# Swapping the places of a search's two products in the attention loop of a two-layer graph network

## The chip, the cores and the metric

The kernel runs on one core of a Trainium2 chip. The metric is the device time of one execution in microseconds (us); lower is better. Five engines work side by side and meet through semaphores: TensorE (PE in the profile; its weight loads, PEld, are shown apart), VectorE (DVE), ScalarE (ACT), GpSimd (POOL) and SyncE (SP), which issues the DMAs.

## The reference

Two layers act on 3327 nodes of 128 features with a dense adjacency matrix. Layer 0 is a masked cosine attention; layer 1 is an attention that has 128 heads of only 8 features each, with the adjacency added twice to the scores. Cut to what matters here:

```python
    def _L1_gnn_ref(x, spatial_encoding, edge_encoding, Wq, Wk, Wv, Wo):
        ...
        q = (x @ Wq.T).reshape(d, n, h)
        k = (x @ Wk.T).reshape(d, n, h)
        v = (x @ Wv.T).reshape(d, n, h)
        a = jnp.einsum('dnh,dmh->dnm', q, k) * scale
        a = a + spatial_encoding + edge_encoding
        a = jax.nn.softmax(a, axis=2)
        out = jnp.einsum('dnm,dmh->dnh', a, v)
...
    x = _layernorm(x + _L0_gnn_ref(x, adj, L0_gnn_beta), axis=-1)
    x = _layernorm(x + _L1_gnn_ref(x, adj, adj, L1_gnn_Wq, L1_gnn_Wk, L1_gnn_Wv, L1_gnn_Wo), axis=-1)
```

Here d is 128 (the heads of layer 1), n is 3327 and h is 8. Every head has its own 3327 x 3327 matrix of scores, each row of which goes through a softmax. The softmax is made safe by subtracting, from each query's scores, the largest product of that query with any key. Finding this largest product is called the search below.

## The kernel before

**Tiling.** The nodes are padded to 3328, which is 26 tiles of 128 (`T`). Queries are taken in blocks of three tiles (384 queries). There are nine blocks; the first eight are full, and the ninth has two tiles. Heads are taken four at a time, so there are 32 groups. One block with one group is a unit; there are 9 x 32 = 288 units, the first 256 of them in full blocks. A unit goes through the 26 key tiles, one step of the main loop (L901) for each. That is 7,488 steps, 6,656 of them in full blocks.

**Rows of the array.** A head's 8 features, split into high and low parts, take 32 rows. Head a of the group lies in rows 32a to 32a+31 (`rows`, L239), so matmuls of different heads use different row groups of TensorE and run side by side. Matmuls of one head queue up in its row group.

**What one step computes.** Scores are made with keys on the partitions and queries along the free axis, for four heads. Two heads go into the two banks of `eb`, the other two into two tiles `ea`.

- `shifts` (L829, matmul at L832) starts a bank with the negated maximum of each query.
- `scores` (L836, L838) adds the products of keys and queries.
- For `eb`, ACT takes the exponential (L938), and POOL multiplies the result by the exponential of twice the adjacency (L939).
- For `ea`, TensorE adds twice the adjacency itself (`add_adj`, L815, eight matmuls at L819 that use all rows and 32 columns each), and ACT takes the exponential of each head (L963).
- `weigh` (L847, eight matmuls at L849) multiplies the weights of two steps before with the values and accumulates them in `acc`.

**The search.** While a unit is weighed, the maxima of later units are searched for (33 steps ahead). In full blocks each step has two pieces of it, made by `max_steps` (L242): a *pair*, which is one chunk of 512 keys against 128 queries for two heads (`max_pair`, L284: two matmuls into the two banks of tile `m2`, and one DVE reduction at L291 over 1024 columns), and a *single*, the same for one head (`max_single`, L306: one matmul into tile `m1`, one reduction at L312 over 512 columns). The single's head is never one of the pair's two. Chunk 6 holds only 256 keys, so a pair or single of that chunk is made of products of two query tiles or units (L302, L316). The searched unit's finished maxima are turned into shifts by `shift_parts` and three small transposes (`shift_turn`, L805), which three of each 26 steps carry.

**Banks.** All eight PSUM banks are in use: `ea` has two (a new step needs both back), `eb` two, `m2` two, `m1` one, `acc` one. So each product waits for the reader of the step before: the pair's matmuls for the reduction L291, the single's for L312, the shifts of `eb` for L938 and those of `ea` for L963.

**Order.** The four engines run in the order in which the program is written (`manual_schedule`); nothing reorders it. In a full-block step, TensorE's order is: shifts of `eb`, pair, scores of `eb`, shifts of `ea`, single, scores of `ea`, (shift turns), `add_adj`, `weigh`. DVE reduces the pair and then the single. The heads of `eb` (`hs_b`, L923) are the two that the pair doesn't use, so shifts and scores of `eb` have two row groups and the pair has the other two.

In the ninth block's search (`behind`, L914) both pieces are singles and follow the scores of `eb`.

Of the kernel before, what the change touches and what calls it, by code (L numbers as in the profile page):

```python
# [46 lines left out]
def gnn_two_layers(  # L47
# [188 lines left out]
    class Banks:  # L236
        pair = single = None
# [85 lines left out]
    def search(step):  # L323
        if step is not None:
            (max_pair if len(step[1]) == 2 else max_single)(*step)
# [16 lines left out]
    def max_step(k):  # L342

        i, j = divmod(k, 2 * T)
        if 2 * i >= NU:
            return None
        if j == 0:
            steps[i] = max_steps(2 * i, 2 * i + 1)
        return steps[i][j]

    def first_max(k):
        pair, single = max_step(k)
        max_pair(*pair)
        max_single(*single)
        if k == T:
            shift_parts(us[0])
# [415 lines left out]
    with ExitStack() as at:  # L772
# [15 lines left out]
        def load_values(u):  # L788

            u.vt = vts[u.i % 3]  # L790
            for first, n, rows in ((0, 112, T), (112, P - 113, T), (P - 1, 1, N - (P - 1) * T)):
                nc.sync.dma_start(
                    u.vt.rearrange("p g t r -> p g (t r)")[first : first + n, :, : rows * R9],
                    bass.AP(
                        tensor=v_s.tensor,
                        offset=v_s.offset + (4 * u.g * N + first * T) * R9,
                        ap=[[T * R9, n], [N * R9, 4], [1, rows * R9]],
                    ),
                )
            u.cx = sm.tile([P, QB], BF16, name="cx")  # L800

        def shift_turn(u, q, dst, start):
            for h in range(4):
                r = slice(32 * h, 32 * h + 32)
                nc.tensor.matmul(  # L805
                    dst[r],
                    parts[u.i % 2][:, q, h],
                    unit,
                    start=start,
                    stop=True,  # L810
                    tile_position=(0, 32 * h),
                    skip_group_check=True,
                )
# [58 lines left out]
        with tc.manual_schedule(  # L872
            engines={
                mybir.EngineType.PE,
                mybir.EngineType.Activation,
                mybir.EngineType.DVE,
                mybir.EngineType.Pool,
            }
        ):
            for i in range(2):  # L880
                load_values(us[i])
            for k in range(k_first, T + AHEAD):
                first_max(k)
            pp = at.enter_context(tc.tile_pool(name="at_p", bufs=6))
            seen = []
            acc = ps_o.tile([P, 512], F32, name="acc")
            nc.vector.memset(acc, 0.0)
            one = fix.tile([P, P], BF16, name="one")
            nc.vector.tensor_copy(one, ones)

            def new_a():
                return [ps_a.tile([P, 512], F32, name="ea") for _ in range(2)]

            e = ps_b.tile([P, 2, 512], F32, name="eb")
            for q in range(QT):
                shift_turn(us[0], q, e[:, 0, q * P : (q + 1) * P], True)
            nc.scalar.copy(us[0].cx, e[:, 0, :QB])  # L897

            todo = []
            turn = []  # L900
            for s in range(NU * T + LAG):  # L901
                i, j = divmod(s, T)
                u = us.get(i)
                if u is not None:
                    if j == 2 and i + 2 < NU:
                        load_keys(new_unit(i + 2))
                        load_queries(us[i + 2], own.tile([P, QB], F32R, name="qx"))
                        load_values(us[i + 2])
                    if j == 12 and i + 4 < G4:
                        gather(i + 4)  # L910
                    k = s + T + AHEAD
                    pair, single = max_step(k) or (None, None)

                    behind = pair is not None and len(pair[1]) == 1  # L914
                    if behind and Banks.pair is not None:
                        Banks.pair = None
                        search_banks.close()
                        ps_n = at.enter_context(tc.tile_pool(name="at_n", bufs=3, space=PSUM))
                        Banks.single = lambda: ps_n.tile([P, 512], F32, name="m3")
                    if behind:  # L920
                        hs_b = pair[1] + single[1]
                    else:
                        hs_b = (2, 3) if pair is None else tuple(  # L923
                            h for h in range(4) if h not in pair[1]
                        )
                    hs_a = tuple(h for h in range(4) if h not in hs_b)

                    e_b = ps_b.tile([P, 2, 512], F32, name="eb")
                    b01 = [e_b[:, x] for x in range(2)]
                    shifts(u, b01, hs_b)  # L930
                    if not behind:
                        search(pair)
                    scores(u, j, b01, hs_b, True)
                    if behind:
                        search(pair)
                        search(single)
                    pt_b = pp.tile([P, 2, QB], F32, name="pb")
                    nc.scalar.activation(pt_b[:, :, : u.nq], e_b[:, :, : u.nq], AF.Exp)  # L938
                    nc.gpsimd.tensor_tensor(  # L939
                        pt_b[:, :, : u.nq],  # L940
                        pt_b[:, :, : u.nq],
                        eT[:, j, : u.nq].unsqueeze(1).to_broadcast([P, 2, u.nq]),
                        ALU.mult,
                    )
                    e_a = new_a()
                    shifts(u, e_a, hs_a)
                    if not behind:
                        search(single)
                    scores(u, j, e_a, hs_a, False)
                    free = e_a[0][:, QB:]  # L950
                    x = us.get(i + 1)
                    copies = []
                    q = j - (T - 4)
                    if x is not None and 0 <= q < x.nt:
                        shift_turn(x, q, free, False)
                        copies.append(
                            lambda: nc.scalar.copy(x.cx[:, q * P : (q + 1) * P], free)
                        )
                    pt_a = pp.tile([P, 2, QB], F32, name="pa")
                    for h, e in enumerate(e_a):  # L960
                        add_adj(e, u, j)
                    for h, e in enumerate(e_a):
                        nc.scalar.activation(pt_a[:, h, : u.nq], e[:, : u.nq], AF.Exp)  # L963
                    for f in copies:
                        f()
                    if x is not None and not x.b:
                        order_keys(x, j)
                        if j == T - 1:
                            keep_keys(x)
                    pts = {}  # L970
                    for x in range(2):
                        pts[hs_a[x]], pts[hs_b[x]] = pt_a[:, x], pt_b[:, x]
                    todo.append((u, j, pts))
                    seen.append((pt_a, pt_b))
                    if len(seen) == 2:
                        a, b = seen.pop(0)
                        if s % 4 == 2:
                            met = sm.tile([P, 1], F32, name="met")
                            nc.scalar.activation(met, b[:, 0, 0:1], AF.Identity, bias=a[:, 0, 0:1])  # L979

                    if k % (2 * T) in (T, 2 * T - 1):
                        v = us.get(k // (2 * T) * 2 + (k % (2 * T) > T))
                        if v is not None:
                            shift_parts(v)
                if s >= LAG:
                    w = todo.pop(0)
                    weigh(*w)
                    if w[1] == T - 1:
                        take(us.pop(w[0].i))

                if turn and turn[0][0] <= s:
                    exp_adj_tile(*turn.pop(0)[1:])
                if u is not None and i + 1 < NU and units[i + 1][0] != u.b:
                    load_adj_tile(u.b + 1, j)
                    turn.append((s + 5, u.b + 1, j))
# [98 lines left out]
```

## Time and profile before

| | |
|---|---|
| median of 3 runs (lowest to highest) | 15163.88 us (15163.75 to 15168.83) |
| profiled execution | 15166.36 us |
| its span, from the first to the last instruction | 15164.6 us |
| mean granted TensorE clock | 0.996 of full speed |
| first shift of `eb` in the timeline | 774.61 us |
| first `eb` shift of the ninth block (128x256 tiles) in the timeline | 13908.37 us |
| mean step in the full blocks: 13133.76 us over 6,656 steps | 1.973 us |

Two costs per step, from the table of the costliest groups (mean of one, over the whole program):

| engine, line | work | mean ns |
|---|---|---|
| DVE L291 | reduction of a pair | 1226 |
| DVE L312 | reduction of a single | 682 |
| ACT L938 | exponential of `eb` | 788 |
| ACT L963 | exponential of one head of `ea` (two a step) | 479 |
| POOL L939 | product with the adjacency's exponential | 1766 |

A busy share says little here: PE is 99% busy, DVE 92%, POOL 91% and ACT 86%. Since matmuls overlap and their ends are modelled, a busy PE is not one at its peak. What sets the length of a step has to be read from the order of events inside a step.

### The profile page before, as it was taken

The page shows a single profiled execution, that of the slowest core. Times are in us where ns is not written, and L with a number is a line of the kernel's source. Part 1 is how long each engine was busy: PE and PEld are TensorE (multiplying, and loading weights), DVE is VectorE, ACT ScalarE, POOL GpSimd, SP SyncE. Part 2 cuts the span into 40 slices and gives each one's busy share as a digit, 9 for nine tenths or more (in the row PEclk, how much of TensorE's full clock was granted, in tenths as well). Part 3 has the DMA queues.
Part 4 walks back from the last instruction along what each step waited for, and adds up shares of the span by engine and source line. Part 5 has one row for each costly group of instructions (what it writes and reads, how often), then busy time and mean ns, then how long its engine had stood idle before and what let it go on. Part 6 is the DMA issues. An engine that isn't in the chain of part 4 may idle for free.

```text
span 15164.6 us, 489663 instructions
## 1 busy us (share of the span) xinstructions
PE 15016.7 (99%) x210460; PEld 6659.0 (44%) x210460; DVE 13878.7 (92%) x16267; ACT 13046.2 (86%) x27285; POOL 13765.4 (91%) x8925
## 2 busy tenths in 40 slices
PE   7899999999999999999999999999999999999999
PEld 5544444444444444444444444444444444444556
DVE  8899999999999999999999999999999999998997
ACT  7699999888888888888888888888888888888887
POOL 3489999999999999999999999999999999999998
PEclk9999999999999999999999999999999999999999
DMA  5622221111111111111111111111111111111222
GB/s 199 216 96 104 98 97 60 47 53 47 57 50 47 54 51 50 53 47 52 55 47 53 47 59 49 47 53 52 54 49 47 53 54 50 50 47 62 66 70 86
DMA packets 548935, 996.33 MB, mean 66 GB/s; under 512 B 147881, under 2 KB 492454, under 8 KB 500422
## 3 DMA queue, kind: packets, MB, share of 16 engines
q1 hardware_dynamic: 546758, 965.00, 19.3%
q8 instruction: 1648, 27.00, 0.7%
q14 instruction: 529, 4.33, 0.1%
HBM read 826.75 MB, written 192.54 MB: 67 GB/s over the span
## 4 chain that ended last, share of the span: by engine, by line
PE 96%; DVE 1%; ACT 1%; issue 1%; POOL 1%; DMA 0%; SPq 0%; DVEq 0%; POOLq 0%; ACTq 0%
PE acc L849 31%; PE ea L819 22%; PE m L276 17%; PE eb L832 13%; PE ea L832 8%; PE ea L838 1%; PE ea L805 1%; PE eb L838 1%; PE sc L394 1%; PE acc L527 0%; PE tp L135 0%; DVE kx L489 0%; ACT aT L439 0%; DVE pt L519 0%; DVE kx L486 0%
## 5 line engine op out<-in xcount | busy, mean ns | idle before, releaser
L939 POOL TENSOR_TENSOR pb<-pb,eT 128x768 f32<-128x768 f32 (+1 forms) x7488 | 13167.5, 1766 | 829.9 <-ACT pb L938 471.5
L291 DVE TENSOR_REDUCE mx<-m 128x2 f32<-128x1024 f32 x6369 | 7809.5, 1226 | 918.5 <-PE eb L838 565.5
L938 ACT ACTIVATE pb<-eb 128x768 f32<-128x768 f32 (+1 forms) x7488 | 5904.2, 788 | 1823.0 <-PE eb L838 1604.7
L276 PE MATMUL m<-kn,qx 32*128 32x512 f32 (+1 forms) x23128 | 6533.6, 463 | 0.0
L963 ACT ACTIVATE pa<-ea 128x384 f32<-128x384 f32 (+1 forms) x14976 | 6348.2, 479 | 10.0 <-PE ea L819 1.4
L849 PE MATMUL acc<-pb,vt 128*9 128x384 f32 (+1 forms) x29952 | 5905.0, 474 | 0.2 <-POOL pb L939 0.2
L849 PE MATMUL acc<-pa,vt 128*9 128x384 f32 (+1 forms) x29952 | 5904.7, 474 | 0.0
L312 DVE TENSOR_REDUCE mx<-m 128x1 f32<-128x512 f32 x7139 | 4803.3, 682 | 88.2 <-PE m L276 28.4
L832 PEld LDWEIGHTS <-one 3*128 3x128 bf16 x29952 | 1395.1, 91 | 5543.1 <-issue 4647.4
L819 PE MATMUL ea<-aT,two 128*32 128x384 bf16 (+1 forms) x59904 | 3715.2, 325 | 0.0
L838 PE MATMUL eb<-qx,kn 32*128 32x384 f32 (+1 forms) x13312 | 3026.3, 451 | 0.0
L838 PE MATMUL ea<-qx,kn 32*128 32x384 f32 (+1 forms) x13312 | 2940.1, 435 | 0.0
L276 PEld LDWEIGHTS m<-kn,qx 32*128 32x128 f32 x23128 | 2725.1, 182 | 221.7 <-DVE mx L312 0.7
L832 PE MATMUL ea<-cx,one 3*128 3x384 bf16 (+1 forms) x14976 | 2706.4, 325 | 0.0
L832 PE MATMUL eb<-cx,one 3*128 3x384 bf16 (+1 forms) x14976 | 2464.8, 326 | 0.7 <-ACT cx L897 0.6
L849 PEld LDWEIGHTS acc<-pa,vt 128*9 128x9 f32 x29952 | 1417.3, 91 | 394.0
L849 PEld LDWEIGHTS acc<-pb,vt 128*9 128x9 f32 x29952 | 1417.1, 91 | 393.5 <-POOL pb L939 0.9
L819 PEld LDWEIGHTS <-two 128*32 128x32 bf16 x59904 | 937.2, 94 | 1388.3 <-issue 1152.7
L838 PEld LDWEIGHTS eb<-qx,kn 32*128 32x128 f32 x13312 | 1277.3, 189 | 0.0
L838 PEld LDWEIGHTS ea<-qx,kn 32*128 32x128 f32 x13312 | 1230.6, 182 | 8.3 <-issue 0.4
L316 DVE TENSOR_REDUCE mx<-m 128x2 f32<-128x512 f32 x1148 | 778.6, 683 | 6.1 <-PE m L276 1.1
L979 ACT ACTIVATE met<-pb,pa 128x1 f32<-128x1 f32 x1872 | 563.6, 301 | 0.1
(131 smaller groups left out, 6005.0 us busy)
## 6 DMA issues: line engine op xcount, KB each, us to landing
kn<-kp_s SPq DMA_DIRECT2D x512, 832.0 KB
vt<-v_s SPq DMA_DIRECT2D x288, 409.5 KB
kn<-kq_s SPq DMA_DIRECT2D x64, 832.0 KB
qx<-qp_s SPq DMA_DIRECT2D x1016, 48.0 KB
kn<-in_adj_dram SPq DMA_DIRECT2D x25, 1663.5 KB
qp_s<-qn_s SPq DMA_DIRECT2D x64, 416.0 KB
kp_s<-kx SPq DMA_DIRECT2D x32, 832.0 KB
kq_s<-kn_s SPq DMA_DIRECT2D x64, 415.9 KB
```

Of the source, the lines that this page charges most:

```text
L276: nc.tensor.matmul(dst, u.qx[rows(a), q * P : (q + 1) * P], u.km[rows(a), k0:k1], start=True, stop=True,)
L291: nc.vector.tensor_reduce(u.mx[:, h, qs[0], c], m, axis=AX.X, op=ALU.max)
L312: nc.vector.tensor_reduce(u.mx[:, a, qs[0], c : c + 1], m, axis=AX.X, op=ALU.max)
L316: nc.vector.tensor_reduce(u.mx[:, a, qs[0] : qs[1] + 1, c], m.rearrange("p (q k) -> p q k", q=2), axis=AX.X, op=ALU.max,)
L819: nc.tensor.matmul(e[r, : u.nq], two[:, r], aT[:, j, : u.nq], start=False, stop=True, tile_position=(0, 32 * c), skip_group_check=True,)
L832: nc.tensor.matmul(e[:, : u.nq], one[r], u.cx[r, : u.nq], start=True, stop=False, skip_group_check=True)
L838: nc.tensor.matmul(e[:, : u.nq], u.kx[rows(a), j * P : (j + 1) * P], u.qx[rows(a), : u.nq], start=False, stop=stop, skip_group_check=True,)
L849: nc.tensor.matmul(acc[32 * h : 32 * h + H + 1, : u.nq], u.vt[:, h, j], pts[h][:, : u.nq], start=(j == 0), stop=(j == T - 1), tile_positio ...
L938: nc.scalar.activation(pt_b[:, :, : u.nq], e_b[:, :, : u.nq], AF.Exp)
L939: nc.gpsimd.tensor_tensor(pt_b[:, :, : u.nq], pt_b[:, :, : u.nq], eT[:, j, : u.nq].unsqueeze(1).to_broadcast([P, 2, u.nq]), ALU.mult,)
L963: nc.scalar.activation(pt_a[:, h, : u.nq], e[:, : u.nq], AF.Exp)
L979: nc.scalar.activation(met, b[:, 0, 0:1], AF.Identity, bias=a[:, 0, 0:1])
```

## The change

In full blocks the two pieces of the search change places in a step, and the heads of `eb` change with them. The single now follows the shifts of `eb`, the pair follows those of `ea`. `eb` holds the heads of the pair, `ea` the other two, one of which is the single's. TensorE's order becomes: shifts of `eb`, single, scores of `eb`, shifts of `ea`, pair, scores of `ea`, (shift turns), `add_adj`, `weigh`. DVE reduces the single and then the pair. The number of instructions, their sizes, the banks and the DMAs stay as they were. The ninth block's search and the steps with no search are as before.

```diff
                     if behind:
                         hs_b = pair[1] + single[1]
                     else:
-                        hs_b = (2, 3) if pair is None else tuple(
-                            h for h in range(4) if h not in pair[1]
-                        )
+                        hs_b = (2, 3) if pair is None else pair[1]
                     hs_a = tuple(h for h in range(4) if h not in hs_b)
...
                     shifts(u, b01, hs_b)
                     if not behind:
-                        search(pair)
+                        search(single)
                     scores(u, j, b01, hs_b, True)
...
                     shifts(u, e_a, hs_a)
                     if not behind:
-                        search(single)
+                        search(pair)
                     scores(u, j, e_a, hs_a, False)
```

## The prediction

> **What bounds the kernel now.** I read the page's busy shares first, then the chain of work that ended last, then two ordinary steps in the timeline, and last the rows of the reductions and their waits.
>
> ```profile
> span 15164.6 us, 489663 instructions
> ...
> PE 15016.7 (99%) x210460; PEld 6659.0 (44%) x210460; DVE 13878.7 (92%) x16267; ACT 13046.2 (86%) x27285; POOL 13765.4 (91%) x8925
> ...
> PE acc L849 31%; PE ea L819 22%; PE m L276 17%; PE eb L832 13%; PE ea L832 8%; PE ea L838 1%; PE ea L805 1%; PE eb L838 1%; PE sc L394 1%; PE acc L527 0%; PE tp L135 0%; DVE kx L489 0%; ACT aT L439 0%; DVE pt L519 0%; DVE kx L486 0%
> ```
>
> The chain names PE for 96%, yet 17% of it stands on the search (L276), whose matmuls run beside others. The timeline shows why. Columns: start and length in us, engine, line, operation, idle time before it.
>
> ```profile
> 7500.66 0.68 DVE L312 TENSOR_REDUCE mx<-m 128x1 f32<-128x512 f32 x1
> ...
> 7500.90 0.50 PE L276 MATMUL m<-kn,qx 32*128 32x512 f32 x2
> ...
> 7501.40 0.18 PEld L276 LDWEIGHTS m<-kn,qx 32*128 32x128 f32 x1
> ...
> 7501.44 1.23 DVE L291 TENSOR_REDUCE mx<-m 128x2 f32<-128x1024 f32 x1
> ...
> 7501.82 0.12 PEld L819 LDWEIGHTS <-two 128*32 128x32 bf16 x8 [0.23 <-issue]
> ...
> 7502.58 0.68 DVE L312 TENSOR_REDUCE mx<-m 128x1 f32<-128x512 f32 x1
> ...
> 7502.90 0.34 PE L832 MATMUL eb<-cx,one 3*128 3x384 bf16 x2
> ...
> 7503.31 0.18 PEld L276 LDWEIGHTS m<-kn,qx 32*128 32x128 f32 x1
> ...
> 7503.45 1.23 DVE L291 TENSOR_REDUCE mx<-m 128x2 f32<-128x1024 f32 x1 [0.18 <-PE eb L838]
> ...
> 7503.49 0.81 ACT L938 ACTIVATE pb<-eb 128x768 f32<-128x768 f32 x1 [0.22 <-PE eb L838]
> ```
>
> The reader is to see that the single's weight load (7501.40) starts 0.06 after the preceding single's reduction ends (7500.66 + 0.68 = 7501.34), and again 7503.31 against 7503.26. Though no row names it as a wait, this load waits for bank `m1` in each step; everything behind it on PE (scores of `ea`, `add_adj`, `weigh`, the next step) waits too. Followed on, this is a loop that closes after two steps: load to first `add_adj` load 0.42 (7501.40 to 7501.82); to the next step 1.08 (7502.90); to the pair's reduction 0.55 (7503.45), the pair's matmuls being made in between; to the single's reduction 1.14 (7502.58 - 7501.44); its length 0.68; back to the load 0.05. Sum 3.92, 1.96 a step. The mean full-block step is (13908.37 - 774.61) / 6656 = 1.973 us; the shift turns (L805, three steps in 26) explain the rest. DVE idles (0.18 above) and so does ACT: neither is the bound alone. PE unhindered is faster: a step from 8003.74 to 8005.61 takes 1.87. What bounds is the loop through both.
>
> **The change, part by part.** It concerns the steps whose search is in full blocks: 6,656 less the 33 by which the search runs ahead, 6,623 steps or 3,311 rounds of the loop. One ns in a round is 3.3 us in all.
>
> *Instruction counts* stay: three search products, two reductions, the same scores. The moved pieces issue only loads, matmuls and reductions, and no DMA; SP's and POOL's queues are passed by nothing.
>
> *The wait.* It moves. The pair's load, now ahead of the scores of `ea`, waits for the reduction of the preceding pair, which is now second on DVE. Behind it stand the same scores, `add_adj` and `weigh`; ACT's L963 waits for them. The single's bank is free early: its reduction ends about 0.55 + 0.68 = 1.23 after the step's start, 0.7 before it is wanted. Before, the pair's had 1.9 - 1.78 = 0.1 to spare. That slack was on no path, so it is worth nothing.
>
> *The new round*, link by link:
> 1. Step start to first reduction (single): was 0.55 with two products, of which the second is issued 3 ns after the first. With one I take 3 ns less.
> 2. Reduction to reduction. Old: 1141 to the single's start + 681 = 1822 ns. New: the single frees DVE 84 ns before its end is shown (back-to-back reductions of the behind steps overlap by that), so 681 - 84 = 597 to the pair's start, and 1226: 1823. Change +1 ns.
> 3. End of reduction to load: 0.05 both times.
> 4. Load to `add_adj`: was 0.42 with one product and two scores in flight. Now it's two products and two scores, as the first half of a step had before: the second product is issued 3 ns later. I take +3.
> 5. `add_adj` to the next step: 1.08, untouched.
>
> Links 1 and 4 aren't shown in their new form; their bounds come from the scores' own rows. Scores issued beside two search products (`eb`, L838) average 464 ns, those beside one (`ea`) 443 to 444 in the steps between 3,000 and 13,000 us. So one product fewer may be worth 0 to 21 ns in link 1, one more may cost 0 to 21 in link 4. I choose 3 for both, as the two loads of a pair start 3 ns apart and last 181 ns like a single's: they load side by side. Round: -3 + 1 + 3 = +1 ns, +3 us in all; bounds -20 to +22 ns, -66 to +73 us.
>
> *Chunk 6.* Two steps in 52 have a pair of four 256-column products. In the second half of the step they may delay the scores of `ea`. In such a step before, the second two loads start 0.11 after the first, and the exponential of `eb` came 0.025 late. Bound 0 to 0.08 on one round in 26: 0 to 10 us; I take 5.
>
> *Costed at nothing.* (a) The pair's product must be ready when the single's reduction ends. It is ready 0.49 + 0.05 after its load; that load comes 0.40 to 0.54 into the step, so 0.94 to 1.08, against 0.55 + 0.60 = 1.15 at which DVE is free. The cover is 0.07 to 0.2 (before it was over 0.6). If the load came later than 0.6, each such step would lose the excess. (b) ACT's L938 waits for `eb` with 0.22 idle before it; a few ns more or less there are covered. The loop through ACT (first `ea` shift after both L963) takes 1.88 a step; if that cover went, it would still lie below 1.973. (c) POOL gets other heads, same size: L939 lasts 1.83 a step in these blocks, 0.14 under the step.
>
> A rule is weighed here. The Trainium skill (TensorE: Matmul & The Clock Gate, Part 3: Packing small matmuls, "The cost: per-tile semaphore tail") says that a group of matmuls packed in row tiles ends later by some 4.7 ns for each tile, and 26.3 for each semaphore increment. It speaks against the pair in link 4 (+4.7, an estimate from that page) and for the single in link 1 (-4.7); increments are as many as before. By it the round would be +1 ns as well, whereas the trace's score rows allow 21 on either side alone. No run here shows the figure per increment.
>
> Sum: 15164.6 + 3 + 5 = 15172.6 us of span. The profiled execution lasted 15166.36, 1.8 more than its span, and the median of the runs is 2.5 below that. So 15163.9 + 8 = 15172 in terms of the median.
>
> **The rivals.**
>
> *A, slower: the fourth row tile stretches the drain.* `add_adj` uses all rows, so it can't start before the last product has left. If two products and two scores end 21 ns later than one and two, and link 1 returns only its 3, the round is +19 ns: 63 us, with chunk 6 at its bound 10, so 15,237. It decides from +10 ns in link 4. For it: 464 against 443 ns. Against it: the scores of `eb` also wait for their shifts, which may be the whole difference. The same side holds the case of (a), a pair that comes too late: 50 ns in every second step would be 166 us. The cover speaks against it.
>
> *B, faster: the wait goes away.* If the pair's bank came back before PE wants it, PE and ACT would run at their own 1.88: 6623 x (1.973 - 1.88) = 616 us less, 14,548. For it: the single's bank is really freed early. Against it: DVE ends its second reduction at 0.55 + 1.82 after the step's start in either order, and one of the two products stands where it must wait for that.
>
> *C, faster: a lighter first half.* One product fewer ends the first half 21 ns sooner and link 4 pays only 3: the round is -17 ns, 56 us less, with chunk 6 at 0: 15,108. For and against: the same rows as for A, read the other way.
>
> **How the numbers follow.** I hold a change of under 0.2% (30 us, about what a measurement of this kernel can tell from no change) the likeliest at 0.55, because both orders close the same round; A with its side case 0.28; B 0.07; C 0.10. So faster 0.17, same 0.55, slower 0.28. The time is the likeliest case's, 15,172. Its own range is 15,145 to 15,195; the range asked for reaches to C and A: 15,110 to 15,240, which leaves out B, the late pair and the far ends, below 2 in 10.
>
> **What would show it.** In the changed trace the pair's loads start 0.05 after L291 ends in nearly each step (right) or at 0.35 into the step with no wait (B). DVE's L291 follows L312 with no idle time (right) or waits for PE (the late pair). Pair's load to `add_adj`: 0.42 to 0.43 (right), 0.44 and more (A). Start to L312: 0.54 to 0.55 (right), 0.53 (C). The mean step stays at 1.973 within 0.004. I would be wrong altogether if the loop weren't what bounds, so that the order of the reductions matters through something else, such as a row group that the new order keeps busy across the change to `add_adj`.

## The result and the profile after

Over 20 runs of each kernel the median went from 15168.58 us (15163.75 to 15173.33) to 15190.7 us (15186.16 to 15194.13). The ratio is 1.0015, with a 95% interval of 1.0009 to 1.0021. So the kernel became slower by some 22 us. That is clear of noise, though less than the 0.2% that the forecast counted as a change. The profiled execution's span is 15187.9 us, at the same granted clock, 0.996.

The page of the changed kernel: the span, and the groups of the two reductions (count, then busy us, mean ns of one, idle time of the engine before it).

```profile
span 15187.9 us, 489661 instructions
...
L291 DVE TENSOR_REDUCE mx<-m 128x2 f32<-128x1024 f32 x6369 | 7744.0, 1216 | 0.1
...
L312 DVE TENSOR_REDUCE mx<-m 128x1 f32<-128x512 f32 x7139 | 4860.9, 690 | 888.6 <-PE eb L838 486.5
```

The same two groups on the page of the kernel before:

```profile
L291 DVE TENSOR_REDUCE mx<-m 128x2 f32<-128x1024 f32 x6369 | 7809.5, 1226 | 918.5 <-PE eb L838 565.5
...
L312 DVE TENSOR_REDUCE mx<-m 128x1 f32<-128x512 f32 x7139 | 4803.3, 682 | 88.2 <-PE m L276 28.4
```

The idle time of DVE has moved from the pair (L291, 918.5 us before) to the single (L312). L291 now runs directly behind L312, with 0.1 us of idle time in the whole program. So the pair's product is never late. A reduction that starts after an idle stretch lasts some 10 ns longer than one that follows another: L291 went from 1226 to 1216, L312 from 682 to 690, and the sum of the two stayed at 1.91 us.

The timeline of two plain steps (start and length in us):

```profile
6911.92 1.22 DVE L291 TENSOR_REDUCE mx<-m 128x2 f32<-128x1024 f32 x1
...
6912.81 0.34 PE L832 MATMUL eb<-cx,one 3*128 3x384 bf16 x2
...
6913.19 0.18 PEld L276 LDWEIGHTS m<-kn,qx 32*128 32x128 f32 x2
...
6913.35 0.69 DVE L312 TENSOR_REDUCE mx<-m 128x1 f32<-128x512 f32 x1 [0.21 <-PE eb L838]
...
6913.62 0.12 PEld L819 LDWEIGHTS <-two 128*32 128x32 bf16 x8 [0.24 <-issue]
...
6913.96 1.22 DVE L291 TENSOR_REDUCE mx<-m 128x2 f32<-128x1024 f32 x1
...
6914.71 0.34 PE L832 MATMUL eb<-cx,one 3*128 3x384 bf16 x2
...
6915.23 0.18 PEld L276 LDWEIGHTS m<-kn,qx 32*128 32x128 f32 x2
```

The pair's loads (x2, 6913.19) come 0.05 after the preceding pair's reduction ends (6911.92 + 1.22 = 6913.14), and again at 6915.23 against 6915.18. So the wait moved as forecast. Steps of 1.90 and some 2.0 us still alternate: as the loop closes after two steps, two chains run interleaved, one from each even step to the next even one and one over the odd steps.

I measured the five links of the two-step loop over the plain steps of both traces (over 3,000 each, without shift turns, chunk 6 and the negated maximum):

| link, mean ns | before | after |
|---|---|---|
| step start to the first reduction | 546 | 537 |
| first reduction's start to the second's end | 1822 | 1824 |
| second reduction's end to the load | 54 | 54 |
| load to the first `add_adj` load | 425 | 429 |
| `add_adj` to the next step | 1088 | 1088 |
| round of two steps | 3935 | 3932 |

A plain round is 3 ns *shorter*: over 3,311 rounds about 11 us less. The loss must lie elsewhere. The search's list of steps repeats after 52 steps (two units; such a period is called a group of 52 steps below), so I averaged the step length by place in it, from 0 to 51. A group takes 102.586 us before and 102.777 after: 0.191 more, times 127.4 groups is 24 us, the whole difference. Up to place 24 the two kernels run level (the running sum of differences is 0.005). At place 25 the step is 0.152 longer, at place 28 it is 0.160 longer, and the steps behind them, on the two chains, give only part of that back.

The timeline of the changed kernel at these places:

```profile
6930.42 0.34 PE L832 MATMUL eb<-cx,one 3*128 3x384 bf16 x2
...
6930.92 0.40 PEld L276 LDWEIGHTS m<-kn,qx 32*128 32x128 f32 x4
...
6931.51 0.12 PEld L819 LDWEIGHTS <-two 128*32 128x32 bf16 x8 [0.19 <-issue]
...
6932.60 0.34 PE L832 MATMUL eb<-cx,one 3*128 3x384 bf16 x2
...
6932.84 0.18 PEld L276 LDWEIGHTS m<-kn,qx 32*128 32x128 f32 x2
...
6932.95 0.19 PEld L276 LDWEIGHTS m<-kn,qx 32*128 32x128 f32 x2
...
6933.74 1.22 DVE L302 TENSOR_REDUCE mx<-m 128x4 f32<-128x1024 f32 x1
...
6934.47 0.34 PE L832 MATMUL eb<-cx,one 3*128 3x384 bf16 x2
...
6935.07 0.24 DVE L330 TENSOR_REDUCE neg<-mx 128x12 f32<-128x84 f32 x1
6935.23 0.68 DVE L312 TENSOR_REDUCE mx<-m 128x1 f32<-128x512 f32 x1
...
6935.82 1.22 DVE L291 TENSOR_REDUCE mx<-m 128x2 f32<-128x1024 f32 x1
...
6937.09 0.18 PEld L276 LDWEIGHTS m<-kn,qx 32*128 32x128 f32 x2
```

Two things are to be seen. First, place 25 (6930.42): the pair is of chunk 6, four products of 256 columns, whose loads take 0.40 together. From its first load to `add_adj` it is 0.59 us (6930.92 to 6931.51), where a plain pair needs 0.43. At place 26 (6932.60) the pair is of chunk 6 too, but its loads come early, 0.24 into the step, with no wait for the bank, and the second two follow the first two by 0.11. Second, place 27 (6934.47): the negated maximum (L330, the first operation of `shift_parts`) now stands directly behind the chunk-6 pair (L302, ends 6934.96), whose result it reads. It starts 0.11 after that end. An independent reduction starts 0.08 before the end of the one ahead. The single then starts 0.76 into its step (6935.23) and not 0.54, the pair ends later, and the pair's load of place 28 comes 0.56 into that step (6937.09 - 6936.53). Before the change, the single stood between the completing pair and the negated maximum. There the latter starts 0.09 before the single's shown end (6924.04 + 0.68 = 6924.72) and falls into what was idle time of DVE:

```profile
6922.89 1.23 DVE L302 TENSOR_REDUCE mx<-m 128x4 f32<-128x1024 f32 x1 [0.17 <-PE eb L838]
6924.04 0.68 DVE L312 TENSOR_REDUCE mx<-m 128x1 f32<-128x512 f32 x1
6924.63 0.23 DVE L330 TENSOR_REDUCE neg<-mx 128x12 f32<-128x84 f32 x1
```

### The profile page after: what moved, and what is told of

Same layout as the page of the kernel before. It is cut to its first block, busy times and chain, and to the rows that moved or that the text cites. A ratio compares the mean times of both kernels' runs of the same rounds, so it can differ in the third digit from the quotient of the medians.

```text
span 15187.9 us, 489661 instructions
## 1 busy us (share of the span) xinstructions
PE 15035.9 (99%) x210460; PEld 6701.0 (44%) x210460; DVE 13894.0 (91%) x16267; ACT 13059.1 (86%) x27285; POOL 13763.5 (91%) x8925
## 4 chain that ended last, share of the span: by engine, by line
PE 95%; ACT 2%; DVE 1%; issue 1%; POOL 0%; DMA 0%; SPq 0%; DVEq 0%; POOLq 0%; ACTq 0%
PE acc L849 30%; PE ea L819 22%; PE m L276 14%; PE eb L832 13%; PE ea L832 8%; PE eb L838 4%; PE ea L838 1%; PE ea L805 1%; PE sc L394 1%; ACT pa L961 1%; ACT pb L936 0%; PE acc L527 0%; PE tp L135 0%; DVE kx L489 0%; ACT aT L439 0%
## 5 line engine op out<-in xcount | busy, mean ns | idle before, releaser
L291 DVE TENSOR_REDUCE mx<-m 128x2 f32<-128x1024 f32 x6369 | 7744.0, 1216 | 0.1
L312 DVE TENSOR_REDUCE mx<-m 128x1 f32<-128x512 f32 x7139 | 4860.9, 690 | 888.6 <-PE eb L838 486.5
L832 PE MATMUL ea<-cx,one 3*128 3x384 bf16 (+1 forms) x14976 | 3958.0, 321 | 0.4
L832 PEld LDWEIGHTS <-one 3*128 3x128 bf16 x29952 | 1493.2, 91 | 5399.5 <-issue 4650.0
L316 DVE TENSOR_REDUCE mx<-m 128x2 f32<-128x512 f32 x1148 | 789.8, 693 | 154.1 <-PE eb L838 84.5
```

The source lines that it names most:

```text
L291: nc.vector.tensor_reduce(u.mx[:, h, qs[0], c], m, axis=AX.X, op=ALU.max)
L312: nc.vector.tensor_reduce(u.mx[:, a, qs[0], c : c + 1], m, axis=AX.X, op=ALU.max)
L316: nc.vector.tensor_reduce(u.mx[:, a, qs[0] : qs[1] + 1, c], m.rearrange("p (q k) -> p q k", q=2), axis=AX.X, op=ALU.max,)
L832: nc.tensor.matmul(e[:, : u.nq], one[r], u.cx[r, : u.nq], start=True, stop=False, skip_group_check=True)
```

## The experiments

The eleven kernels ran in three groups, each beside runs of the kernel before on the same chip, with medians of 15162.02 (the first four), 15165.55 (the next four) and 15165.0 us (the last three). The last group's kernels are told where they belong.

**Theory 1: two rare events, not the plain step.** The first run gives the chunk-6 pairs their old places and heads back.

```diff
+                        first, second = single, pair
+                        if pair is not None and pair[3] == 6:
+                            hs_b = tuple(h for h in range(4) if h not in pair[1])
+                            first, second = pair, single
...
-                        search(single)
+                        search(first)
...
-                        search(pair)
+                        search(second)
```

> The changed kernel, but in the 2 of 52 steps whose pair is chunk 6 the pair keeps its old place and the heads their old banks. Theory 1 (the plain round is about 3 ns shorter, and the loss comes from the four products of a chunk-6 pair in the second half, 0.15 us a group of 52 steps, and from the negated maximum that then follows that pair at once, 0.16): both are gone, a group takes 102.55 to 102.60 us against 102.59 before and 102.78 after, so 15,164 to 15,171. Rival A (every pair in the second half stretches the drain): at most 2 of 52 steps change, 15,188 to 15,191.

Measured: 15262.69 us, ratio 1.0067 (1.0054 to 1.0079). It is 100 us slower than before, and neither theory said that. Its timeline at places 25 and 27:

```profile
6965.81 1.22 DVE L291 TENSOR_REDUCE mx<-m 128x2 f32<-128x1024 f32 x1
6966.59 0.34 PE L832 MATMUL eb<-cx,one 3*128 3x384 bf16 x2
6967.09 0.40 PEld L276 LDWEIGHTS m<-kn,qx 32*128 32x128 f32 x4 [0.40 <-DVE mx L291]
...
6967.73 1.23 DVE L302 TENSOR_REDUCE mx<-m 128x4 f32<-128x1024 f32 x1 [0.69 <-PE m L276]
...
6971.12 0.34 PE L832 MATMUL eb<-cx,one 3*128 3x384 bf16 x2
6971.35 0.23 DVE L330 TENSOR_REDUCE neg<-mx 128x12 f32<-128x84 f32 x1
6971.48 0.18 PEld L276 LDWEIGHTS m<-kn,qx 32*128 32x128 f32 x1 [0.28 <-DVE mx L312]
```

At the switch from the new order to the old, the pair stands at the start of a step, while the pair of the step before was reduced last. Its bank comes back only 0.50 into the step (6967.09 - 6966.59), and the weight loads and DVE both stand still (0.40 and 0.69 idle). At the switch back the single waits in the same way (6971.48). So the order matters after all where it changes. A step's first product finds its bank free when it is the one that DVE reduced first in the step before. Either order does that when it is kept throughout, and this mixture does not.

The second run leaves the order alone and issues the negated maximum with its three parts one step later.

```diff
-                    if k % (2 * T) in (T, 2 * T - 1):
-                        v = us.get(k // (2 * T) * 2 + (k % (2 * T) > T))
+                    kk = k - 1
+                    if kk % (2 * T) in (T, 2 * T - 1):
+                        v = us.get(kk // (2 * T) * 2 + (kk % (2 * T) > T))
```

> The changed kernel, but the negated maximum and its three parts are issued one step later. Theory 1: the 0.16 us at the 28th step of a group and the 0.04 at its first go, the 0.15 of the four-product pair stays on one of the two interleaved chains: 15,177 (15,170 to 15,184). Rival: the four-product pair alone costs, the negated maximum nothing: 15,190. Rival: the negated maximum alone costs: 15,160.

Measured: 15165.12 us, 3 above its runs of before (ratio 1.0002, 0.9992 to 1.0011). The loss shrank from 22 to 3 us. The range of theory 1 was set against 15168.58, so it meant 1 to 15 us above before: 3 lies in it, near its low end. Of its two rivals, the one that meant 21 above is out; the one that meant 9 below is 12 us off, but still inside the interval (12 below to 17 above). In its timeline at place 28 the same reduction starts 0.09 *before* the pair ends (6925.13 + 1.22 = 6926.35) and the single is on time, 0.53 into the step:

```profile
6925.13 1.22 DVE L291 TENSOR_REDUCE mx<-m 128x2 f32<-128x1024 f32 x1
...
6926.06 0.34 PE L832 MATMUL eb<-cx,one 3*128 3x384 bf16 x2
...
6926.26 0.23 DVE L330 TENSOR_REDUCE neg<-mx 128x12 f32<-128x84 f32 x1
...
6926.59 0.69 DVE L312 TENSOR_REDUCE mx<-m 128x1 f32<-128x512 f32 x1
```

The third run has both edits.

> The changed kernel with both edits: chunk-6 pairs in their old places and the negated maximum one step later. Theory 1: the plain round's 3 ns are left over 3,311 rounds, 10 us, and the small stall of the negated maximum that the kernel before has too at the first step of a group: 15,152 to 15,160, faster than before. If the two places weren't the whole loss, 15,165 or more.

Measured: 15255.1 us, ratio 1.0061 (1.0048 to 1.0074). That is 93 us above before, against 101 in the first run: the switches cost nearly the same here, and the expectation fell with the first run's. The fourth run is the kernel before with the second run's edit.

> The kernel before, with the negated maximum one step later. Theory 1: the stall of 0.07 us at the first step of a group goes, on one of the two chains, 0.03 to 0.07 a group of 52 steps: 15,159 to 15,165. If the negated maximum costs nothing there: 15,168.

Measured: 15156.84 us, 5 less than before (ratio 0.9997, 0.9988 to 1.0005). The range expected was set against 15168.58, so it meant 4 to 10 us less; 5 fits. The sign isn't shown at this interval.

**Theory 2: the negated maximum behind the pair it depends on is most of the loss, the four-product pair a small rest.** Two runs put the scores of `ea` ahead of the pair, so that they don't queue behind its four products; the second has the later negated maximum as well.

```diff
-                    if not behind:
-                        search(pair)
                     scores(u, j, e_a, hs_a, False)
+                    if not behind:
+                        search(pair)
```

> The changed kernel, with the scores of ea issued ahead of the pair instead of behind it. Theory 2 (the negated maximum behind the pair it depends on is most of the loss; the four-product pair of chunk 6 is a small rest): plain steps stay, since the pair decides the link to add_adj anyway; the four-product step's 0.60 us from load to add_adj falls to about 0.51; the time is that of before plus 10 to 24 us. Rival (the four-product pair is the loss): before plus 0 to 5 us.

Measured: 15183.81 us, 18 above before (ratio 1.0013, 1.0004 to 1.0022), within theory 2's 10 to 24 and outside the rival's 0 to 5. The link of the four-product step fell to 0.53 (the expectation said 0.51); the plain link stayed at 429 ns.

> The changed kernel with both: scores of ea ahead of the pair, negated maximum one step later. Theory 2: the run with the negated maximum later alone stood 3 us above before; what is left there of the four-product pair, up to 0.1 us a group of 52 steps, goes: before less 10 to before plus 3. If scores that don't wait for the pair shorten the plain round too, more than 15 us below before.

Measured: 15162.5 us, 3 below before (ratio 0.9998, 0.9989 to 1.0007). The later negated maximum was worth 21 us here, and 19 without the scores' edit. This is the best form of the changed order. It can't be told from the kernel before, nor from that kernel with the later negated maximum.

Theory 2 is right about the event and wrong about the rest. The run of the changed kernel with the later negated maximum stood 3 us above before, that of the kernel before with the same edit 5 below: by these medians, whose intervals overlap, the change without the event is 8 us slower, though its plain rounds gain 11. That leaves some 19 us for the four-product pairs, no small rest. The traces of these two runs agree: averaged by place, the running sum of their differences is -0.05 us at places 21 to 24 and +0.10 at places 29 to 34. That is 0.15 a group, 19 us over 127 groups.

The suspected cost was then put into the kernel before: in the one step of 52 whose chunk-6 pair completes a unit, the negated maximum is reduced right behind that pair.

```diff
                     if not behind:
                         search(pair)
+                        if pair is not None and k % (2 * T) == T:
+                            negated(us[k // (2 * T) * 2])
```

> The kernel before with the suspected cost put in: in the step whose chunk-6 pair completes a unit (one step in 52) the negated maximum is reduced right behind that pair, ahead of the single; the three parts stay where they were. Theory 2: it starts some 0.10 us after the pair's end instead of 0.08 before it, and delays the single and so the next step's load by 0.35 us on one of the two chains: 0.2 to 0.35 us a group, before plus 25 to 45 us. Rival (the dependency costs nothing, the reduction's 0.16 us alone counts and the chain's slack takes it): before plus 0 to 10 us.

Measured: 15210.49 us, 45 above before (ratio 1.0031, 1.0019 to 1.0042), at the upper end of theory 2's 25 to 45. Its timeline:

```profile
6945.24 1.23 DVE L302 TENSOR_REDUCE mx<-m 128x4 f32<-128x1024 f32 x1 [0.19 <-PE eb L844]
...
6946.57 0.24 DVE L330 TENSOR_REDUCE neg<-mx 128x12 f32<-128x84 f32 x1
...
6946.73 0.68 DVE L312 TENSOR_REDUCE mx<-m 128x1 f32<-128x512 f32 x1
...
6947.47 0.18 PEld L276 LDWEIGHTS m<-kn,qx 32*128 32x128 f32 x1 [0.42 <-DVE mx L312]
```

The same 0.10 stands between the pair's end (6946.47) and L330, and PE's next single waits 0.42 for it. One such event in 52 steps is worth 45 us in the old order. This holds the 0.16 that L330 takes ahead of the single (6946.73 - 6946.57) as well as the 0.19 of the dependency; the run doesn't part them.

**What the two halves of the change do alone.** First the heads without the places, then the places without the heads.

```diff
-                        hs_b = (2, 3) if pair is None else tuple(
-                            h for h in range(4) if h not in pair[1]
-                        )
+                        hs_b = (2, 3) if pair is None else pair[1]
```

> The kernel before, with the change's heads alone: eb holds the pair's heads, the pair stays behind the shifts of eb, the single behind those of ea. The pair's products now queue in eb's own row groups: 0.25 to the end of the shifts + 0.21 + 0.10 + 0.05 = 0.61 us from step start to the pair's reduction against 0.55, so the round is at least 0.06 longer: 200 us, 15,360; up to 16,000 if the longer first half delays the exponentials of eb as well. If row groups don't matter: 15,165 or so.

Measured: 15998.29 us, ratio 1.0549 (1.0534 to 1.0563).

```diff
-                        hs_b = (2, 3) if pair is None else pair[1]
+                        hs_b = (2, 3) if pair is None else tuple(
+                            h for h in range(4) if h not in pair[1]
+                        )
```

> The changed kernel with the old heads: the places are swapped, eb holds the heads that the pair doesn't use. Single and scores of eb share a row group, and pair and scores of ea share two: 0.07 more to the single's reduction, and 0.16 more from the pair's load to add_adj, since the scores of ea stream behind the pair: 0.23 a round of two steps, 760 us, 15,930 (15,700 to 16,300). If row groups don't matter: 15,190.

Measured: 16016.22 us, ratio 1.0561 (1.0547 to 1.0576). Either half alone costs over 5%. In both, the first reduction starts some 0.61 into a step (0.55 before), L938 at 0.79 (0.59 before), and the load of the second piece to `add_adj` takes 0.60. Products of one row group queue up: the search's and the scores'. In the heads-alone run the pair shares the rows of `eb`, and the single those of one head of `ea`. My 15,360 had counted only the first; the 16,000 given as an upper end was what came, but not for the reason given with it: link 1 grew by 0.07 and link 4 by 0.17, and 0.24 over 3,311 rounds is some 800 of the 833 us. The places-alone run lies in its range.

**Is the loop the bound?** Both kernels with the single's reduction over half of its columns:

```diff
-            nc.vector.tensor_reduce(u.mx[:, a, qs[0], c : c + 1], m, axis=AX.X, op=ALU.max)
+            nc.vector.tensor_reduce(u.mx[:, a, qs[0], c : c + 1], m[:, :256], axis=AX.X, op=ALU.max)
```

> The kernel before, with the single's reduction over the first 256 of its 512 columns (the other half of the chunk is left out of the maximum). If the two-step loop through DVE bounds, a round loses some 0.27 us and the bound passes to PE and ACT at 1.87 to 1.89 a step: 14,560 to 14,640 us. If PE bounds by itself, as its 99% says: 15,165.

Measured: 14735.48 us, ratio 0.9718 (0.9703 to 0.9733).

> The changed kernel with the same edit (half of each single left out of the maximum). If the loop bounds and is the same in both orders, it goes to the same bound: 14,560 to 14,660, within 40 us of the kernel before with that edit. If PE bounds by itself: 15,190.

Measured: 14715.27 us, ratio 0.9703 (0.969 to 0.9717). With no work taken from PE, the times are 430 and 450 us under the kernel before: PE's 99% isn't the bound, the loop through DVE is. The kernel before, with this edit:

```profile
6911.24 0.41 DVE L312 TENSOR_REDUCE mx<-m 128x1 f32<-128x256 f32 x1
6911.42 0.33 PE L832 MATMUL eb<-cx,one 3*128 3x384 bf16 x2
...
6911.77 0.18 PEld L276 LDWEIGHTS m<-kn,qx 32*128 32x128 f32 x1
...
6913.29 0.34 PE L832 MATMUL eb<-cx,one 3*128 3x384 bf16 x2
```

The single's reduction ends at 6911.65, and the load comes 0.12 later, 0.35 into the step: it waits no more, and the step is 1.87. I had expected 14,560 to 14,640, and up to 14,660 for the changed kernel; both came out longer. The median step is 1.880 and 1.871 us, but the mean is 1.905 and 1.902, for two reasons of about equal weight. Steps with shift turns now take up to some 2.01. And in four steps of 52 the first of two chunk-6 singles stood in the step before; the edit leaves its reduction (L316) at full length, so the load waits again, until 0.54 into the step, and the step takes some 2.05 (2.23 at place 25 of the changed kernel). Where the wait is gone the changed order is 20 us ahead. Why is not shown: POOL is 97% busy in both runs between 3,000 and 13,000 us, so POOL may set that step as well as PE.

## Why the prediction was right, and where its steps were not

- *The bound* was right: a loop that closes after two steps, through the single's bank before and the pair's bank after. The half-length reductions show it, and so do the loads 0.05 behind the end of the reduction in both traces.
- *The move of the wait* was right: same round, other bank. Rival B (the wait goes away) was wrong.
- *Links 1 to 5* were right in kind, with the sizes a little off. Link 1 gave 9 ns where I took 3, link 2 cost 2 (I took 1), link 4 cost 4 (I took 3). The plain round changed by -3 ns, not +1, which is -11 us, not +3. Rival A, the stretched drain, was wrong: 4 ns, not 21. Rival C was nearer with its lighter first half, at less than half its 21 ns. The 21 ns themselves were no measure of a product more or less: in the changed kernel the scores of `eb`, now beside one product, still average 464 ns, and those of `ea`, beside two, 440 (3,000 to 13,000 us). The prediction's own doubt, that `eb`'s scores wait for their shifts, fits that better.
- *The cover of (a)* held: L291 lost 0.1 us in all to waits. *(b) and (c)*: the five links account for the plain round without ACT and POOL.
- *Chunk 6* was mis-sized: some 17 to 19 us where I took 5 and allowed 10. I bounded it at 0.08 us for one round in 26, from steps before the change, where the second two loads come 0.11 behind the first. At place 25 they come 0.19 behind, and the link grows by 0.17. It isn't the second half of the step that does this: at place 26, also in the second half, they come 0.11 behind and cost nothing, and in the first experiment, where this pair stood in the first half and waited 0.40 for its bank, the four loads take 0.40 as well. What I took over was the spacing of loads that hadn't waited. The 17 to 19 us are by subtraction (22 measured, 11 gained in the plain rounds, 14 to 16 for the negated maximum), and the two traces without the event give 19; scores ahead of the pair won 4 to 6 of them back. It was not measured alone, as giving these pairs their old places brings the switches in.
- *The sentence on what is behind what* had the other gap. I listed what is queued behind the moved pair on PE, and not what follows it on DVE. There, `shift_parts` reads the pair's own result. That event costs 19 to 21 us when it is taken away from the changed order. Some 5 of them belong to a like stall that the order before has at place 0, where the negated maximum stands directly behind a single whose result it reads; so 14 to 16 came with the change. No term of the sum stood for it.

The total was close (8 us forecast, 22 measured) because a gain that I had put too low and two losses that I had put too low or left out cancelled in part. The direction that was forecast, slightly slower and under 0.2%, came out, but not for the reasons of the sum: that the total came this close is in part luck.

## What to carry to other kernels

When two pieces of work change places, walk through *every* in-order queue that they stand in, and ask of each neighbour whether it now reads what the piece ahead of it has just written; a rare neighbour on the loop that bounds can outweigh a few ns in each step. With single banks, see that the product which a step makes first is the one that was reduced first in the step before: mixing the two orders in 2 of 52 steps cost 101 us here, where either one kept throughout stayed within 22 of the other. An average by place in the program's own period (here 52 steps) finds such events when the plain steps of two traces look alike.

## What the runs showed of the hardware

- On DVE an instruction that doesn't depend on the one ahead starts 0.08 us before that one's shown end; one that reads its result starts 0.10 to 0.11 after it (the negated maximum behind L316 in the trace before, behind L302 and L291 in the trace after). The dependency is worth 0.19 us even inside one engine.
- Four f32 products of 256 columns in two row groups load in 0.30 us where the loads didn't wait for their bank (0.11 between the first two loads and the second two: places 25 and 26 before, place 26 after). They load in 0.40 where they did (0.19 between them: place 25 after, in the second half of a step, and place 25 of the first experiment, in the first half). Why the second two come later there is open.
- PE, busy for 99% of the span, did not set it: in the kernel before, halving the columns of DVE's reduction of the single took 2.8% off the time, with PE's work unchanged.
